# Base's logits inside the W_out products, Cm folded into the state matrices, and a new order of rows, ids and gathers

## The chip, the core and the metric

The kernel runs on one core of a Trainium2 chip. Its engines work side by side, each through its own queue of instructions in order: TensorE (PE, matmuls; PEld is its weight loads), VectorE (DVE), ScalarE (ACT), GpSimd (POOL) and SyncE (SP, which only issues DMA transfers here). The metric is the device time of one launch in microseconds.

## The reference, cut to what matters

There are 8 sequences of 512 tokens with 256 features. Each passes a modulated layer norm and a state-space block, and then a modulated layer norm and a mixture of 8 experts in which each token uses one expert.

```
mod = (silu(c) @ wmod) -> sa, ca, ga, sb, cb, gb      # per sequence; ga, gb kept away from 0
h = layernorm(x) * (1 + ca) + sa
xn = layernorm(h) * gamma + beta;  u, z = split(xn @ W_in.T)
xc = silu(causal_conv4(u) + conv_b)
state_t = state_{t-1} @ A.T + u_t @ Bm.T              # 16 states
y_t = (xc_t + state_t @ Cm) * sigmoid(z_t)
x = x + ga * (h + y @ W_out.T)
h = layernorm(x) * (1 + cb) + sb
logits = h @ wr + br;  gate = p1 / (p1 + p2);  e = argmax(logits)
x = x + gb * gate * (gelu(h @ w1[e] + b1[e]) @ w2[e] + b2[e])
```

All of it is float32. The profile shows one float32 matmul as two instructions, each with its weight load.

## The kernel before, in words

**The plan.** The kernel does not issue instructions as it builds them. A class `Plan` records each one with the tiles it reads and writes, a supposed length and a due time (`nc.due`), and `order` (L191) lays them out as a list schedule: always the instruction that could start first, the earlier due time deciding between equals. The result fixes the order of instructions on every engine's queue, SP's included. What a DMA is supposed to take after its issue stands in `order`: 3.5 us for an indirect one (a gather or scatter on GpSimd's queue), bytes over a shared wire of 300 GB/s for another, and 2.2 us of reach behind either. On the chip, semaphores make an instruction wait for its inputs, and everything behind it on the same engine waits too. Two plans follow each other, the sequences' and the experts'; all of the first is emitted ahead of the second. In the profile nearly every instruction carries the line of the recorder, L159, or L154 for further matmuls of one group.

**The first plan** makes the matrices of `states` and `vectors` and then works on sequence after sequence: `stage_norm` (both layer norms, `xnT`, the normalized rows with features on partitions), `stage_base` (`base` = x + ga h, its transpose `baseT`, W_out times ga as `wb_` with 8 further columns `wr2` that yield logits), `stage_conv`, `stage_out`, `stage_place`. The stages of neighbouring sequences overlap as the plan decides.

The states are computed in chunks of 4 tokens. `stage_conv` puts the inputs of the states into `v` [128, 128] (position in the chunk by state on partitions, chunk on columns), sums over chunks by products `pd`, turns `v` into all states `s` by four products with `lq` (`pst`) and a copy on ScalarE, and does the convolution in `sv`. `stage_out` multiplies `s` with Cm: `cmt` holds four pieces of Cm at partitions 0, 32, 64 and 96, and two products `pc` of 32 rows run side by side. VectorE adds them to `sv` and multiplies by the gate, and `po` is the product with `wb_`: 256 columns of output and 8 of logits. The part of the logits that comes from `base` is a product of its own in `stage_base`, `pl`, copied to `bl` and added to the logits `lg`.

`stage_place` writes the rows `xr` of the sequence to `xp_d` in DRAM (L933, on SP; on ScalarE's queue for the last sequence), next to modulation rows that SP has copied there. It counts each token's place in its expert's list and scatters token numbers to `ids_d` with four indirect DMAs.

**The experts** work in slots of 256 tokens (128 for some) of one expert. `name_tokens` (L1047) loads a slot's token numbers from `ids_d` to `ids` on SP; `expert_of` (L1059) loads the expert's w1, b1, b2 and w2 on SP (2.1 MB); `rows_of` gathers the rows to `xg` on GpSimd's queue; `features` normalizes and modulates them in `hg` and transposes them (`tp`) to `hT`; `layer1` gives `ph` and, through the gelu, `gl`; `layer2` gives `py` and `ot`, which is scattered to the output. The slots 0 to 2 are named after six sequences, when the lists already hold three full blocks, and slot 0's first layer belongs to the first plan. The other slots need all eight sequences: a table on VectorE ends in `ei`, which holds their experts and places. Weights of three slots are fetched ahead (four buffers). The ids of the first four late slots are loaded before the slots' loop `work` (L1313), all others in its first turn.

Of the kernel before, what the change touches and what calls it, by code (L numbers as in the profile page):

```python
# [10 lines left out]
FP = mybir.dt.float32  # L11
I32 = mybir.dt.int32
AF = mybir.ActivationFunctionType
ALU = mybir.AluOpType
# [21 lines left out]
class Plan:  # L36
# [154 lines left out]
    def order(self):  # L191
# [34 lines left out]
        while len(order) < len(ops):  # L226
# [63 lines left out]
def adaln_mamba_moe_kernel(  # L290
# [71 lines left out]

    cmt = cpool.tile([P, P], FP, name="cmt")
    nc.gpsimd.memset(cmt, 0.0)
# [69 lines left out]
    with tc.tile_pool(name="wa", bufs=1) as wa, tc.tile_pool(  # L434
# [32 lines left out]
        for j in range(KI):  # L467
            nc.sync.dma_start(out=cmt[32 * j : 32 * j + DS, :], in_=cm[:, j * P : (j + 1) * P])
# [124 lines left out]
        def states():  # L593
# [16 lines left out]

            lt = wa.tile([DS, CH, P], FP, name="lt")
# [72 lines left out]
            return lq, wb, lm, bw  # L684
# [81 lines left out]
        def stage_base(t):  # L766

            b, xt, bc, h = (t[k] for k in ("b", "xt", "bc", "h"))
            base = h
            nc.gpsimd.tensor_tensor(base, base, rows(bc[:, 2, :]), ALU.mult)  # L770
            nc.gpsimd.tensor_tensor(base, base, xt, ALU.add)
            wb_ = a2.tile([P, KI, D + E], FP, name="wb_")
            nc.gpsimd.tensor_tensor(
                wb_[:, :, 0:D], wo, bc[:, 2, :].unsqueeze(1).to_broadcast([P, KI, D]), ALU.mult
            )
            nc.gpsimd.tensor_copy(wb_[:, :, D:], wr2[:, :, b, :])
            baseT = a2.tile([P, KD, L], FP, name="baseT")
# [11 lines left out]
            t.update(base=base, wb_=wb_, bl=bl)  # L789

        def stage_conv(t):
# [4 lines left out]
            v = a2.tile([P, NC], FP, name="v")  # L796
# [52 lines left out]
            t.update(s=s, sv=sv)  # L849

        def stage_out(t):


            b, xnT, s, sv, base, wb_, bl = (
                t[k] for k in ("b", "xnT", "s", "sv", "base", "wb_", "bl")
# [3 lines left out]
            for g in range(KI // 2):  # L859
                pair = (2 * g, 2 * g + 1)  # L860
                tz, pc = {}, {}
                for j in pair:
                    tz[j] = a3.tile([P, L], FP, name=f"tz_{b}_{j}", tag="tz")
                    with nc.wanting([tz[j]]):
                        px = project(xnT, b, KI + j)
                    nc.scalar.activation(tz[j], px, AF.Tanh, scale=0.5)
                with nc.wanting(done=[sv[:, j, :] for j in pair]), nc.side_by_side():
                    for j in pair:
                        pc[j] = ps_x.tile([P, L], FP, name=f"pc_{b}_{j}", tag="px")
# [4 lines left out]
                for j in pair:  # L874
                    nc.vector.tensor_tensor(sv[:, j, :], sv[:, j, :], pc[j], ALU.add)
                    nc.vector.scalar_tensor_tensor(
                        y2[:, j, :], tz[j], 1.0, sv[:, j, :], ALU.add, ALU.mult
                    )
# [44 lines left out]
        def stage_place(t):  # L923
# [9 lines left out]
            (nc.sync if b < B - 1 else nc.scalar).dma_start(  # L933
# [125 lines left out]
        def expert_of(i, w1t, w2t, b1t, b2t):  # L1059
# [16 lines left out]
            loads(fn, [w1t, b1t, b2t, w2t], [number], 2.5)  # L1076
# [44 lines left out]
        lq, wb, lm, bw = states()  # L1121
        rw, rsum, wr2 = vectors()
        for b in range(B):
# [6 lines left out]
            if b == FEW - 1:  # L1130
# [6 lines left out]
                for i in range(2):  # L1137
# [15 lines left out]
                    epool.tile([P, D], FP, name="b2_0"),  # L1153
# [8 lines left out]
    with tc.tile_pool(name="g", bufs=2) as gp, tc.tile_pool(  # L1162
# [150 lines left out]
        def work(slots, got, begun=None):  # L1313
# [27 lines left out]
        late = slots[NEARLY:]  # L1341
        for i in late[:FIRST]:
            name_tokens(i)
# [65 lines left out]
```

## Time and profile before

| | |
|---|---|
| three runs | 624.2, 630.1, 630.36 us; median 630.1 |
| the profiled execution | 630.57 us, its span 628.8 |
| TensorE | busy 578.3 us, mean granted clock 0.941 |
| VectorE, ScalarE, GpSimd | busy 355.0, 211.5, 212.8 us |
| DMA | 96.72 MB, 154 GB/s over the span |
| setup, then sequences | up to about 62 us, then to 336; first `po` groups of the eight at 77.8, 115.6, 147.7, 183.3, 219.6, 254.1, 289.2, 329.0 us |
| experts | first layer of slot 0 at 336.6, last matmul near 615 us |

The page's first part gives each engine's busy time; the second shows the span in 40 slices, with the clock that was granted to TensorE; the groups and waits give, for an engine's idle time, the instruction or transfer that ended it. A timeline row is start, length, engine, line, operation, output and inputs, with the idle time before it in brackets. In rows of SPq an entry's length is the time that SyncE needed for the issues, not the transfer's.

### The profile page before, as it was taken

The numbers are of one execution on the slowest core, as the hardware profiler recorded it, in microseconds if no ns is written. First come the engines' busy times: TensorE is split into PE (matmuls) and PEld (weight loads), VectorE is DVE, ScalarE is ACT, GpSimd is POOL, SyncE is SP. The second block draws the span as 40 slices with busy tenths as digits, with TensorE's granted clock in tenths as the row PEclk, the third lists the DMA queues.
The fourth block names the chain that finished last, engine by engine and source line by source line (L and its number), as shares of the span: only waits on it lengthen the run. The fifth ranks groups of instructions, "written<-read, shape, count | busy, mean of one in ns | idle before, by whom it ended". The sixth has DMA issues, their size and how long they took to land. (4 is left out here: it accounts for less than half of the span.)

```text
span 628.8 us, 8434 instructions
## 1 busy us (share of the span) xinstructions
PE 578.3 (92%) x2754; PEld 422.4 (67%) x2754; DVE 355.0 (56%) x1101; ACT 211.5 (34%) x408; POOL 212.8 (34%) x335
## 2 busy tenths in 40 slices
PE   5899999999999999999699865899999999999991
PEld 2456565656475665656358755688988988988980
DVE  6869589598968678476396612353342541542210
ACT  2227244354463445351252211121322223322320
POOL 1603562735344364530322312333332233321101
PEclk9859699899989799998999996899999999999996
DMA  8268996220301001010814995999887877882000
GB/s 289 88 165 227 261 269 137 37 75 0 94 0 35 1 2 35 0 36 0 269 44 121 189 203 167 342 389 358 284 276 241 297 242 263 282 303 90 24 4 16
DMA packets 58799, 96.72 MB, mean 154 GB/s; under 512 B 9900, under 2 KB 41966, under 8 KB 58752
## 3 DMA queue, kind: packets, MB, share of 16 engines
q1 hardware_dynamic: 50288, 72.44, 39.2%
q0 software_dynamic: 7936, 23.17, 10.5%
q10 hardware_dynamic: 528, 0.53, 0.8%
q8 instruction: 23, 0.38, 0.3%
q14 instruction: 24, 0.20, 0.2%
HBM read 86.42 MB, written 22.81 MB: 174 GB/s over the span
## 5 line engine op out<-in xcount | busy, mean ns | idle before, releaser
L159 ACT ACTIVATE gl<-ph,b1t 128x256 f32<-128x256 f32 (+1 forms) x152 | 68.6, 451 | 191.9 <-PE ph L154 189.9
L154 PE MATMUL py<-w2t,gl 128*128 128x256 f32 x476 | 108.5, 380 | 0.1
L154 PEld LDWEIGHTS py<-w2t,gl 128*128 128x128 f32 x476 | 90.5, 190 | 12.6 <-issue 0.5
L159 POOL DMA_INDIRECT out<-ot,ids x36 | 38.0, 1055 | 160.2 <-DVE ot L159 151.4
L159 PE MATMUL ph<-hT,w1t 128*128 128x256 f32 (+1 forms) x304 | 85.2, 362 | 0.0
L154 PE MATMUL ph<-hT,w1t 128*128 128x256 f32 (+1 forms) x304 | 84.8, 361 | 0.0
L159 PE MATMUL px<-xnT,wi 128*128 128x512 f32 x128 | 77.4, 689 | 0.0
L159 DVE SCALAR_TENSOR_TENSOR sv<-u,pt,sv 128x512 f32<-128x512 f32 x96 | 71.5, 758 | 4.0 <-ACT sv L159 4.0
L154 PE MATMUL px<-xnT,wi 128*128 128x512 f32 x128 | 71.9, 646 | 0.0
L159 DVE TENSOR_TENSOR ot<-py,b2t 128x256 f32<-128x256 f32 x34 | 14.4, 423 | 92.6 <-PE py L154 92.6
L159 POOL DMA_INDIRECT xg<-xp_d,ids x36 | 37.1, 1031 | 70.6 <-DMA ids<-ids_d 49.5
L154 PEld LDWEIGHTS ph<-hT,w1t 128*128 128x128 f32 x304 | 56.0, 193 | 6.5
L159 PEld LDWEIGHTS ph<-hT,w1t 128*128 128x128 f32 x304 | 55.8, 195 | 5.7
L159 POOL DMA_INDIRECT ids_d<-tok,row x32 | 37.0, 1156 | 54.9 <-DVE row L159 30.6
L154 PEld LDWEIGHTS px<-xnT,wi 128*128 128x128 f32 x128 | 26.9, 210 | 35.1 <-issue 35.1
L159 DVE TENSOR_SCALAR hg<-xg 128x256 f32<-128x256 f32 x36 | 15.0, 418 | 60.0 <-DMA xg<-xp_d,ids 60.0
L159 ACT COPY u<-px 128x512 f32<-128x512 f32 x32 | 18.7, 583 | 69.1 <-PE px L154 69.1
L159 ACT ACTIVATE tz<-px 128x512 f32<-128x512 f32 x32 | 19.1, 596 | 57.8 <-PE px L154 55.1
L159 PEld LDWEIGHTS px<-xnT,wi 128*128 128x128 f32 x128 | 22.5, 205 | 23.6 <-issue 18.0
L159 POOL TENSOR_TENSOR rs<-ve,nhalf 128x4 f32<-128x4 f32 x16 | 20.0, 1250 | 43.5 <-DVE ve L159 23.9
L159 DVE TENSOR_TENSOR xr<-po,h 128x256 f32<-128x256 f32 x32 | 13.5, 423 | 31.0 <-PE po L154 28.4
L159 DVE TENSOR_TENSOR hg<-hg,xg 128x256 f32<-128x256 f32 x72 | 28.6, 421 | 0.9
(360 smaller groups left out, 955.3 us busy)
## 6 DMA issues: line engine op xcount, KB each, us to landing
w1t<-in_w SPq DMA_DIRECT2D x19, 1024.0 KB, 7.6
w2t<-in_w SPq DMA_DIRECT2D x19, 1024.0 KB, 5.9
xp_d<-modb_d SPq DMA_DIRECT2D x8, 1536.0 KB, 29.1
xt<-in_x SPq DMA_DIRECT2D x8, 512.0 KB, 6.9
xp_d<-xr SPq DMA_DIRECT2D x7, 520.0 KB, 3.5
bc<-mod_d SPq DMA_DIRECT2D x7, 384.0 KB, 5.1
b2t<-in_b SPq DMA_DIRECT2D x19, 128.0 KB, 7.3
w<-in_w SPq DMA_DIRECT2D x2, 1024.0 KB, 8.9
```

Source lines behind the costliest of these rows:

```text
L154: me["calls"].append(lambda: getattr(getattr(self.nc, name), op)(*args, **kw))
L159: calls=[lambda: getattr(getattr(self.nc, name), op)(*args, **kw)],
```

## The change

- Indirect DMAs count 9.0 us in the plan, not 3.5.
- `cs` takes the place of `lq` and `s`: the matrices of `states` are multiplied with Cm once, in the setup (four products with 512 columns, four copies on ScalarE), and `pc` is four full products of `cs` and `v` for each quarter of the channels. `cmt` is loaded once, [16, 512]. There are no pairs side by side any more; `v` has three buffers.
- `pl`, `bl` and their copy go; the products of `baseT` and `rw` are accumulated on the last 8 columns of `po`, and `lg` is a copy.
- The last sequence's `xr` is written from SP like the others.
- In the plan, slot 0's weights stand behind the early gathers.
- One late slot's ids are loaded before the loop; in each turn the next slot's ids are loaded ahead of the weights that are fetched in it.

```diff
-                    end += 3.5
+                    end += 9.0
...
-        for j in range(KI):
-            nc.sync.dma_start(out=cmt[32 * j : 32 * j + DS, :], in_=cm[:, j * P : (j + 1) * P])
+        cmt = wa.tile([DS, DI], FP, name="cmt")
+        nc.sync.dma_start(out=cmt, in_=cm)
...
-            i4 = wa.tile([DS, P], FP, name="i4")
-            nc.vector.memset(i4, 0.0)
-            for q in range(P // SP):
-                nc.vector.tensor_copy(i4[:, q * SP : q * SP + DS], i16)
-            pq = ps_s.tile([P, CH, P], FP, name="pq", tag="ps")
+            cs = wa.tile([P, CH, DI], FP, name="cs")
             for i in range(CH):
-                nc.tensor.matmul(pq[:, i], lhsT=lt[:, i, :], rhs=i4, start=True, stop=True)
-            lq = wa.tile([P, CH, P], FP, name="lq")
-            nc.vector.tensor_copy(lq, pq)
+                pq = ps_x.tile([P, DI], FP, name=f"pq_{i}", tag="px")
+                nc.tensor.matmul(pq, lhsT=lt[:, i, :], rhs=cmt, start=True, stop=True)
+                nc.scalar.copy(cs[:, i, :], pq)
...
-            pl = ps_t.tile([P, NT, E], FP, name="pl", tag="tp")
-            bl = a3.tile([P, NT, E], FP, name="bl")
-            with nc.wanting([bl]):
-                for n in range(NT):
-                    for k in range(KD):
-                        nc.tensor.matmul(
-                            pl[:, n, :], lhsT=baseT[:, k, n * P : (n + 1) * P],
-                            rhs=rw[:, k, 0, b, :], start=(k == 0), stop=(k == KD - 1),
-                        )
-            nc.vector.tensor_copy(bl, pl)
...
-            v = a2.tile([P, NC], FP, name="v")
+            v = a3.tile([P, NC], FP, name="v")
...
-            pst = ps_s.tile([P, L], FP, name=f"pst_{b}", tag="ps")
-            s = a2.tile([P, L], FP, name="s")
-            with nc.wanting([s]):
-                for i in range(CH):
-                    nc.tensor.matmul(
-                        pst.rearrange("p (c i) -> p i c", i=CH)[:, i, :], lhsT=lq[:, i, :], rhs=v,
-                        start=True, stop=True,
-                    )
-            nc.scalar.copy(s, pst)
...
-                        nc.tensor.matmul(
-                            pc[j], lhsT=cmt[j * SP : (j + 1) * SP, :],
-                            rhs=s[j * SP : (j + 1) * SP, :], start=True, stop=True,
-                        )
...
+            for j in range(KI):
+                tz = a3.tile([P, L], FP, name=f"tz_{b}_{j}", tag="tz")
+                with nc.wanting([tz]):
+                    px = project(xnT, b, KI + j)
+                nc.scalar.activation(tz, px, AF.Tanh, scale=0.5)
+
+                pc = ps_x.tile([P, L], FP, name=f"pc_{b}_{j}", tag="px")
+                with nc.wanting(done=[sv[:, j, :]]):
+                    for i in range(CH):
                         nc.tensor.matmul(
+                            pc.rearrange("p (c i) -> p i c", i=CH)[:, i, :],
+                            lhsT=cs[:, i, j * P : (j + 1) * P], rhs=v, start=True, stop=True,
                         )
+                nc.vector.tensor_tensor(sv[:, j, :], sv[:, j, :], pc, ALU.add)
...
                             po, lhsT=y2[:, j, n * P : (n + 1) * P], rhs=wb_[:, j, :],
-                            start=(j == 0), stop=(j == KI - 1),
+                            start=(j == 0), stop=False,
+                        )
+
+                    for k in range(KD):
+                        nc.tensor.matmul(
+                            po[:, D:], lhsT=baseT[:, k, n * P : (n + 1) * P],
+                            rhs=rw[:, k, 0, b, :], start=False, stop=(k == KD - 1),
                         )
...
-                nc.vector.tensor_tensor(lg[:, n, :], po[:, D:], bl[:, n, :], ALU.add)
+                nc.vector.tensor_copy(lg[:, n, :], po[:, D:])
...
-            (nc.sync if b < B - 1 else nc.scalar).dma_start(
+            nc.sync.dma_start(
                 out=xp_d[b * L : (b + 1) * L, 0:OWN].rearrange("(n p) c -> p n c", p=P), in_=xr
...
-        def expert_of(i, w1t, w2t, b1t, b2t):
+        def expert_of(i, w1t, w2t, b1t, b2t, behind=()):
...
-            loads(fn, [w1t, b1t, b2t, w2t], [number], 2.5)
+            loads(fn, [w1t, b1t, b2t, w2t], [number, *behind], 2.5)
...
-                    epool.tile([P, D], FP, name="b2_0"),
+                    epool.tile([P, D], FP, name="b2_0"), pre,
...
+                if n + ahead + 1 < len(slots):
+                    name_tokens(slots[n + ahead + 1])
                 if n + ahead < len(slots):
                     got.append(fetched(slots[n + ahead]))
...
-                    for i in late[FIRST:]:
-                        name_tokens(i)
...
-        late = slots[NEARLY:]
-        for i in late[:FIRST]:
-            name_tokens(i)
+        name_tokens(slots[NEARLY])
```

More of the change, by code (lines that the diff above doesn't have):

```diff
@@ L361, in adaln_mamba_moe_kernel @@
     at = cpool.tile([DS, STEPS, 2, DS], FP, name="at")
-    cmt = cpool.tile([P, P], FP, name="cmt")
-    nc.gpsimd.memset(cmt, 0.0)
     brt = cpool.tile([P, E], FP, name="brt")
@@ L682, in states @@
             nc.vector.tensor_copy(bw[:, :, 0:DS], pb)
-            return lq, wb, lm, bw
+            return cs, wb, lm, bw
         def stats(src, b, which, rs=None, nm=None):
@@ L778, in stage_base @@
             to_features(baseT, base, None, None, f"b{b}")
-            pl = ps_t.tile([P, NT, E], FP, name="pl", tag="tp")
-            bl = a3.tile([P, NT, E], FP, name="bl")
-            with nc.wanting([bl]):
-                for n in range(NT):
-                    for k in range(KD):
-                        nc.tensor.matmul(
-                            pl[:, n, :], lhsT=baseT[:, k, n * P : (n + 1) * P],
-                            rhs=rw[:, k, 0, b, :], start=(k == 0), stop=(k == KD - 1),
-                        )
-            nc.vector.tensor_copy(bl, pl)
-            t.update(base=base, wb_=wb_, bl=bl)
+            t.update(base=base, wb_=wb_, baseT=baseT)
         def stage_conv(t):
@@ L848, in stage_conv @@
                 nc.scalar.activation(cv, cv, AF.Silu)
-            t.update(s=s, sv=sv)
+            t.update(v=v, sv=sv)
         def stage_out(t):
-            b, xnT, s, sv, base, wb_, bl = (
-                t[k] for k in ("b", "xnT", "s", "sv", "base", "wb_", "bl")
+            b, xnT, v, sv, base, wb_, baseT = (
+                t[k] for k in ("b", "xnT", "v", "sv", "base", "wb_", "baseT")
             )
             y2 = sv
[L859 to L869, printed above, removed]
+            for j in range(KI):
[6 more added lines that the diff above has]
+                    for i in range(CH):
@@ L870, in stage_out @@
                         nc.tensor.matmul(
-                            pc[j], lhsT=cmt[j * SP : (j + 1) * SP, :],
-                            rhs=s[j * SP : (j + 1) * SP, :], start=True, stop=True,
-                        )
[L874 to L877, printed above, removed]
-                    )
+                            pc.rearrange("p (c i) -> p i c", i=CH)[:, i, :],
@@ L880, in stage_out @@
+                            lhsT=cs[:, i, j * P : (j + 1) * P], rhs=v, start=True, stop=True,
+                        )
+                nc.vector.tensor_tensor(sv[:, j, :], sv[:, j, :], pc, ALU.add)
+                nc.vector.scalar_tensor_tensor(
+                    y2[:, j, :], tz, 1.0, sv[:, j, :], ALU.add, ALU.mult
+                )
             xr = rowp.tile([P, NT, OWN], FP, name="xr")
@@ L888, in stage_out @@
                             po, lhsT=y2[:, j, n * P : (n + 1) * P], rhs=wb_[:, j, :],
-                            start=(j == 0), stop=(j == KI - 1),
+                            start=(j == 0), stop=False,
+                        )
+                    for k in range(KD):
+                        nc.tensor.matmul(
+                            po[:, D:], lhsT=baseT[:, k, n * P : (n + 1) * P],
+                            rhs=rw[:, k, 0, b, :], start=False, stop=(k == KD - 1),
                         )
                 nc.vector.tensor_tensor(x1[:, n, :], po[:, 0:D], base[:, n, :], ALU.add)
-                nc.vector.tensor_tensor(lg[:, n, :], po[:, D:], bl[:, n, :], ALU.add)
+                nc.vector.tensor_copy(lg[:, n, :], po[:, D:])
             rs, nm = stats(x1, b, 2, xr[:, :, D], xr[:, :, D + 1])
@@ L1120, in adaln_mamba_moe_kernel @@
         PERIOD = 36.0
-        lq, wb, lm, bw = states()
+        cs, wb, lm, bw = states()
         rw, rsum, wr2 = vectors()
```

## The prediction

> **What bounds the kernel now.** I read the page first, then the table of stretches, then TensorE's timeline around every stretch in which it idled or ran slowly, then those of SyncE and the DMA queues. A page line gives busy time, share and instructions; PEclk is the granted clock in tenths for 40 slices of 15.7 us.
>
> ```profile
> span 628.8 us, 8434 instructions
> ...
> PE 578.3 (92%) x2754; PEld 422.4 (67%) x2754; DVE 355.0 (56%) x1101; ACT 211.5 (34%) x408; POOL 212.8 (34%) x335
> ...
> PEclk9859699899989799998999996899999999999996
> ```
>
> TensorE is busy 92% and no other engine above 56%, so time is lost where TensorE idles or is slowed: the dips in PEclk. There are three kinds.
>
> **First**, half clock while TensorE is busy. The table of stretches, 3.41 us each (busy time of TensorE, its weight loads, VectorE, ScalarE, GpSimd; then PEclk, DMA share, GB/s):
>
> ```profile
> 144.44:147.85 3.41, 3.41 (x24) 2.71 (x23) 3.41 (x8) 0.60 (x1) 0.68 (x3) 1.00 0.01 0
> 147.85:151.26 3.41, 3.41 (x18) 2.90 (x17) 1.11 (x9) 3.37 (x7) 1.10 (x3) 1.00 0.00 0
> ...
> 175.16:178.57 3.41, 3.41 (x28) 2.56 (x24) 3.41 (x11) 1.62 (x3) 2.60 (x6) 0.99 0.01 0
> 178.57:181.98 3.41, 3.41 (x7) 1.18 (x4) 2.39 (x8) 0.00 (x0) 1.18 (x6) 0.51 0.00 0
> ```
> and TensorE's timeline in the third (start, length, operation):
> ```profile
> 174.60 0.69 PE L159 MATMUL pc<-s,cmt 32*128 32x512 f32 x1
> ...
> 175.66 0.33 PE L159 MATMUL tp_a<-ident,xn 128*128 128x128 f32 x1
> ...
> 176.15 0.29 PE L159 MATMUL pl<-rw,baseT 128*128 128x8 f32 x2
> ...
> 177.94 0.69 PE L159 MATMUL pc<-s,cmt 32*128 32x512 f32 x1
> ```
>
> The stretch ahead of the drop is busy throughout, but filled with `pl` (8 columns) and `pc` (32 rows). Drops of this part start at 65.9, 110.3, 178.6, 212.7, 250.2 and 284.4, whole multiples of 3.41 us apart, each behind `pl` next to `pc` (the first behind `pl` next to `pr`, 64 columns). From 144.44 to 147.85, `pl` has 1.7 of 3.41 us with px beside it, and no drop follows: half a stretch of thin products is borne, four fifths are not (246.8 to 250.2: 1.75 of `pl`, 1.06 of `pc`).
>
> **Second**, the logits of sequence 6, 298 to 311 us (bracket: idle before, releaser):
>
> ```profile
> 302.31 1.05 POOL L159 DMA_INDIRECT xg<-xp_d,ids  x1 [18.80 <-DMA ids<-ids_d]
> ...
> 307.31 1.05 POOL L159 TENSOR_TENSOR xr<-ve,nhalf 128x4 f32<-128x4 f32 x1
> ...
> 309.37 0.41 DVE L159 TENSOR_SCALAR hg<-xg 128x256 f32<-128x256 f32 x1 [11.05 <-DMA xg<-xp_d,ids]
> ...
> 311.27 0.39 PE L159 MATMUL pd<-v,lm 32*32 32x120 f32 x2 [4.72 <-DVE v L159]
> ```
>
> The plan counts 3.5 us for a gather; these landed after 8.0 (median). So GpSimd stands before its gathers with the pow that VectorE needs queued behind them, VectorE stands before `hg`, and TensorE idles for v.
>
> **Third**, the passage to the experts:
>
> ```profile
> 345.71 0.42 ACTq L159 DMA_DIRECT2D xp_d<-xr  x1
> ...
> 360.99 0.70 PE L159 MATMUL py<-w2t,gl 128*128 128x256 f32 x2 [2.61 <-DMA w2t<-in_w]
> ...
> 368.83 0.33 SPq L1052 DMA_DIRECT2D ids<-ids_d  x1
> ...
> 373.53 15.05 SPq L1052 DMA_DIRECT2D ids<-ids_d  x14
> ...
> 383.62 0.47 PE L159 MATMUL tp<-ident,hg 128*128 128x128 f32 x1 [11.79 <-DVE hg L159]
> ...
> 400.90 0.45 PE L159 MATMUL tp<-ident,hg 128*128 128x128 f32 x1 [3.02 <-DVE hg L159]
> ```
>
> Slot 3's ids are read only at 368.8, when the last scatters (issued to 348.9) are in, after up to 19.7 us. Then 14 id loads hold SyncE until 388.6, ahead of slot 4's weights. The last xr lands after 23.0 us from ScalarE's queue; the other seven take 3.5 from SyncE's. From 420 to 610 TensorE has no gap.
>
> **The change, part by part.** The profiled execution took 630.57 us (span 628.8 and 1.8 around it), 0.5 above the median of the runs, 630.1.
>
> *Cm folded in.* Before, per sequence: `pst`, 8 instructions from 172.68 to 173.57, 0.89, and `pc` twice 1.06 (174.60 to 175.66): 3.01. After: 16 products of two instructions, shaped like pst's, 32 x 0.111 = 3.56. So +0.55, times 8: **+4.4**, all on TensorE. ScalarE loses eight copies of 0.585 and v reaches pc without it; ScalarE is 34% busy: 0. v gets a third buffer for its longer life. The Trainium skill speaks against this step: its page TensorEngine Tiling (Array Packing), section Overview, has up to four products of at most 32 rows share the array. By that factor pc would have cost 8 x 0.43 / 4 = 0.86 and the step 8 x (3.56 - 0.89 - 0.86) = +14.5; the trace has 1.06 for two products of a pair, and decides.
>
> *Setup.* `pq` (8 instructions, 1.08 us from 55.77) becomes 8 of 512 columns at px's pitch of 0.43: 3.44, **+2.4**; 0 if it falls into a gap, +5 at the half clock of 32 to 45 us. VectorE is rid of i4 and the lq copy (0.68), ScalarE gets four copies of 0.58, four cm loads (3.07 us of SyncE) become one. None of these ends a wait there: 0.
>
> *Base's logits in po.* The 16 instructions (176.15 to 177.94) move between the po's at the same 0.11 each: 0, bounds -1 (a group start of 0.1 less per sequence) and +2 (0.06 more per output tile). VectorE's bl copy goes (8 x 0.18) and an add becomes a copy, hidden under its idle 44%. baseT now lives until po, as wb_ of two buffers does already: 0.
>
> *The clock.* `pl` is spread, 0.45 us behind each 1.77 of po (a fifth thin), and pc is dense, so no stretch of `pl` beside thin `pc` is left. Slow times: 10.4 us from 65.9, 6.9 from 212.7, 3.4 at the four others; half of each is lost: 5.2 + 3.45 + 4 x 1.7 = 15.4. I take **-13**, since `pr` stays thin in the first; bounds 0 and -15.4.
>
> *3.5 to 9.0.* A scatter, an id load and a gather follow each other, so the plan puts the id loads 5.5 us and `hg` 11 us later; hg was 11.05 late. VectorE then does v and pd first, and GpSimd can serve the pow ahead of some gathers. Gone would be 4.72 of idling and 1.7 lost to the half clock from 312. Two gathers may still stand ahead of the pow: **-5**, bounds 0 and -6.4. Slot 0's weights, now planned behind the gathers, fall behind sequence 6's xr (314.3) and land 8.9 later: 323, needed at 336.6: 0. Behind the last xr (345.7) slot 0 would start some 17 later.
>
> *The passage.* xr is emitted on SyncE ahead of slots 1 and 2, so it waits there for VectorE until 345.6, and behind it wait slot 1's weights (issued at 337.1 before), slot 2's and slot 3's ids. 0.52 + 1.05 MB at 380 GB/s (346 to 350: 379, 357) is 4.1 us, plus 1.8 (what a lone xr takes beyond its 1.4): 351.9, needed at 351.1. Wait 0.8. The other 3.15 MB are in at 360; the scatters land 9.0 to 11.8 after 348.9 (those between 165 and 250 us): 361. Only one id load then stands before weights: ids 4.5 more, gather 2.6 + 8.0, hg 1.3: 377.5. TensorE's own work (four groups of 6.95) lasts to 379.7. Slot 3 starts near 381, not 401.4: -20, of which 17.4 is idling (2.61 + 11.79 + 3.02) and the rest slow clock. This cover is 2 us thin and rests on 380 GB/s, where 350 to 368 moved 114 on average with two queues waiting; at 114 the same chain gives 402, +1. I take **-13**, two thirds of the way, bounds -20 and +27 (rival 1). Later id loads go out one slot before their gather: 4.5 + 8.0 fit into a slot of 14, three slots ahead of use: 0.
>
> Sum: 4.4 + 2.4 - 13 - 5 - 13 = -24.2; 630.6 - 24.2 = **606**.
>
> **Rivals.** (1) *Slower: the loads crawl behind xr.* If the scatters and not ScalarE's queue caused the crawl of 350 to 368, it now meets xr and all 4.2 MB of weights, where 3.4 MB were through by 350 before. Slot 3 starts at 346 + 4.72 MB/rate + 15; that outweighs the other terms (-11.2) below 91 GB/s. At 70 (352 to 356 had 66 and 31) it starts at 428, +27: 646. For it: no row shows scatters beside xr and weights in one queue. Against: scatters beside 1.5 MB copies left these 140 to 186 GB/s at 104 to 110.
> (2) *The ids bound the passage anyway*, at 114 GB/s or with landings of 16.6 to 19.7 as now: 630.6 - 11.2, **619**.
> (3) *The drops are not the thin products'.* Then the 13 stay: **619**. Against: six drops of six stand behind them. The Trainium skill, page TensorE: Matmul & The Clock Gate, section Why this matters for your kernels, warns of gaps of over 3 us without matmuls. By that alone these drops would have no cause that the change removes; the trace has TensorE busy 3.41 of 3.41 ahead of them.
> (4) *The plan changes but not the order on the chip*, since queues and semaphores decide: only clock and products count, 630.6 - 13 + 6.8 = **624**.
>
> **Chances.** Forecast 0.56 (its own range 592 to 614); (1) 0.16, of it 0.11 slower and 0.05 unchanged; (2) 0.13; (3) 0.07; (4) 0.08, half of it unchanged. A measurement of this kernel tells about 1%, 6.3 us, from no change. Faster 0.80, within it 0.09, slower 0.11. The range reaches from all gains, 630.6 + 4.4 + 1 - 15.4 - 6.4 - 20 - 2 = 592, to 630, and leaves out mostly the slower part of (1).
>
> **What would show it.** PEclk at 1.00 from 110 to 290; po groups 33 us apart (289.2 - 183.3 is 3 x 35.3 now); no wait of 11 us of VectorE for xg; the last xr landing in under 6 us; no wait of over 4 us at slot 3's tp. Drops behind stretches without thin products, or w1t of slot 1 landing 12 us after the last xr's issue, would prove me wrong.

## The result, and the profile after

| | before | changed |
|---|---|---|
| runs beside each other (four each) | 624.2 to 630.36 us, median 628.4 | 602.82 to 606.44 us, median 605.6 |
| ratio, 95% interval | | 0.962 [0.955, 0.969] |
| profiled execution, its span | 630.57, 628.8 us | 602.82, 601.0 us |

The sum of the prediction came out, 606 against 605.6, but not by its terms. The two profiled executions lie 27.8 us apart and the medians 22.8, because the one before was the slowest of its four and the changed one the fastest; what follows is read from these two, so its parts add up to 5 us more than the medians differ by. The page of the changed kernel:

```profile
span 601.0 us, 8691 instructions
...
PE 563.9 (94%) x2882; PEld 430.1 (72%) x2882; DVE 351.4 (58%) x1087; ACT 210.5 (35%) x404; POOL 209.3 (35%) x334
...
PEclk9779999999999999999999977999999999999996
```

From the fourth slice to the 23rd the clock stands at 9 (nine tenths or more); what is left of the half clock is in the setup (second and third slice) and in the 24th and 25th, the passage to the experts. The table of stretches, with the cuts at the first `po`, the last sequence's `po` and the first `py` of slot 3. Columns: length, then busy time of TensorE, its weight loads, VectorE, ScalarE, GpSimd, then PEclk, DMA share, GB/s. Before:

```profile
0.00:77.75 77.75, 66.67 (x331) 37.26 (x331) 57.57 (x191) 29.29 (x50) 27.44 (x61) 0.82 0.70 206
77.75:328.95 251.20, 243.20 (x1105) 148.37 (x1103) 187.87 (x595) 109.33 (x197) 109.24 (x202) 0.95 0.24 65
328.95:409.69 80.74, 63.33 (x288) 54.46 (x288) 33.51 (x133) 16.12 (x35) 21.26 (x21) 0.92 0.80 204
```

After:

```profile
0.00:71.98 71.98, 63.33 (x335) 35.67 (x335) 56.35 (x184) 31.98 (x55) 25.65 (x60) 0.91 0.71 200
71.98:304.57 232.59, 229.91 (x1215) 156.36 (x1211) 183.74 (x585) 105.09 (x189) 107.17 (x195) 1.00 0.29 78
304.57:381.44 76.87, 65.35 (x304) 55.62 (x303) 38.47 (x145) 16.28 (x34) 23.61 (x29) 0.91 0.76 213
```

The front (the first two rows) is 24.4 us shorter, the passage 3.9, and the steady slots behind it as long as before (219.1 and 219.6). Time lost to the clock is length times one less PEclk, added up over stretches of a quarter of a microsecond, since the column above is rounded: in the front 13.65 + 11.95 before and 6.8 after, so -18.8. Idle time is length less busy time: 11.1 + 8.0 before, 8.65 + 2.7 after, so -7.7. The rest, work, is +2.1.

Not all of the front is firm. Six of the experiments below (e5, e6, e9, e10, e12 and e13) change nothing in the order of the first plan, and their first `po` begins anywhere from 69.98 to 75.84 us, while from there to the last sequence's `po` they all take 232.2 to 232.7. So the 18.6 us between the first and the last `po` (251.2 before, 232.6 after) stand, and the 5.8 us ahead of the first `po` can't be told from the spread of single executions.

The wait in sequence 6 is gone. GpSimd's rows there:

```profile
285.41 1.00 POOL L159 DMA_INDIRECT xg<-xp_d,ids  x1 [0.31 <-issue]
286.44 1.06 POOL L159 TENSOR_TENSOR xr<-ve,nhalf 128x4 f32<-128x4 f32 x1
287.69 1.06 POOL L159 DMA_INDIRECT xg<-xp_d,ids  x1 [0.19 <-issue]
```

The pow (the row with `nhalf`) now stands behind two of the four gathers, and VectorE's `hg` behind the work on v. TensorE waits there under 1 us.

The passage, rows of SyncE's queue, GpSimd, VectorE and TensorE from one timeline (the length of an SPq row is the time of its issues):

```profile
318.68 0.38 SPq L1041 DMA_DIRECT2D w1t<-in_w  x1
...
323.01 0.38 SPq L159 DMA_DIRECT2D xp_d<-xr  x1
...
341.93 1.43 SPq L1028 DMA_DIRECT2D ids<-ids_d  x2
...
352.62 22.88 SPq L1028 DMA_DIRECT2D ids<-ids_d  x13
```

```profile
326.25 0.98 POOL L159 DMA_INDIRECT ids_d<-tok,row  x1 [0.30 <-issue]
...
346.60 1.05 POOL L159 DMA_INDIRECT xg<-xp_d,ids  x1 [11.78 <-DMA ids<-ids_d]
...
357.32 0.41 DVE L159 TENSOR_SCALAR hg<-xg 128x256 f32<-128x256 f32 x1 [13.05 <-DMA xg<-xp_d,ids]
```

```profile
348.54 0.59 PE L154 MATMUL ph<-hT,w1t 128*128 128x256 f32 x2
358.71 0.48 PE L159 MATMUL tp<-ident,hg 128*128 128x128 f32 x1 [9.57 <-DVE hg L159]
...
364.16 1.06 PE L159 MATMUL py<-w2t,gl 128*128 128x256 f32 x2
```

Slot 1's weights go out ahead of xr, not behind it. Slot 3's ids are read at 341.9, 15.7 us after the last scatter's issue (326.25). Its gathers are issued from 346.6 and land 10.7 us later, while the weights of slots 3 and 4 move, at 400 GB/s from 352 on. TensorE stands 9.57 us before slot 3's `tp`, and half clock follows to 368. Slot 2's second layer (`py`, 364.16) stands behind these transposes in TensorE's queue, so it can't fill the wait.

### The profile page after: what moved, and what is told of

Read it like the earlier page. It is cut to its first block, busy times and chain, and to the rows that moved or that the text cites. A ratio compares the mean times of both kernels' runs of the same rounds, so it can differ in the third digit from the quotient of the medians.

```text
span 601.0 us, 8691 instructions
## 1 busy us (share of the span) xinstructions
PE 563.9 (94%) x2882; PEld 430.1 (72%) x2882; DVE 351.4 (58%) x1087; ACT 210.5 (35%) x404; POOL 209.3 (35%) x334
## 5 line engine op out<-in xcount | busy, mean ns | idle before, releaser
L154 PE MATMUL py<-w2t,gl 128*128 128x256 f32 x476 | 109.8, 383 | 0.0
L154 PEld LDWEIGHTS py<-w2t,gl 128*128 128x128 f32 x476 | 91.7, 193 | 12.9
L159 DVE SCALAR_TENSOR_TENSOR sv<-u,pt,sv 128x512 f32<-128x512 f32 x96 | 77.2, 809 | 12.7 <-ACT sv L159 12.4
L154 PE MATMUL ph<-hT,w1t 128*128 128x256 f32 (+1 forms) x304 | 84.2, 359 | 0.0
L159 PE MATMUL px<-xnT,wi 128*128 128x512 f32 x128 | 69.6, 626 | 0.0
L154 PE MATMUL px<-xnT,wi 128*128 128x512 f32 x128 | 65.9, 597 | 0.0
L154 PEld LDWEIGHTS ph<-hT,w1t 128*128 128x128 f32 x304 | 55.6, 191 | 6.3
L159 POOL DMA_INDIRECT xg<-xp_d,ids x36 | 37.8, 1051 | 60.9 <-DMA ids<-ids_d 40.5
L159 POOL DMA_INDIRECT ids_d<-tok,row x32 | 34.8, 1087 | 36.1 <-DVE row L159 13.7
L154 PEld LDWEIGHTS px<-xnT,wi 128*128 128x128 f32 x128 | 24.6, 192 | 31.2 <-issue 31.2
L159 DVE COPY hT<-tp 128x512 f32<-128x512 f32 (+1 forms) x20 | 12.7, 634 | 36.3 <-PE tp L154 28.1
L159 PEld LDWEIGHTS px<-xnT,wi 128*128 128x128 f32 x128 | 21.3, 192 | 16.4 <-issue 14.8
```

Of the source, the lines that this page charges most:

```text
L154: me["calls"].append(lambda: getattr(getattr(self.nc, name), op)(*args, **kw))
L159: calls=[lambda: getattr(getattr(self.nc, name), op)(*args, **kw)],
```

## The experiments

A kernel that moves instructions is ordered anew by the plan, and the order around the passage falls differently each time. So each run is read in two parts: where the last sequence's `po` begins, and how long the span goes on from there.

| kernel | median us | ratio to before, 95% | last po begins | from there |
|---|---|---|---|---|
| before | | | 329.5 | 299.3 |
| changed | 605.6 | 0.962 [0.955, 0.969] | 305.0 | 296.0 |
| e1 logits apart | 651.8 | 1.039 [1.033, 1.045] | 359.2 | 290.9 |
| e2 Cm in pairs | 606.1 | 0.967 [0.961, 0.972] | 310.5 | 293.5 |
| e3 3.5 us | 615.5 | 0.981 [0.975, 0.987] | 315.3 | 297.5 |
| e4 last xr on ScalarE | 600.6 | 0.958 [0.951, 0.965] | 304.9 | 295.0 |
| e5 no last xr write | 599.4 | 0.957 [0.952, 0.961] | 305.1 | 289.7 |
| e6 no last scatters | 593.4 | 0.947 [0.942, 0.951] | 308.8 | 285.3 |
| e7 orders only | 616.9 | 0.985 [0.981, 0.990] | 324.8 | 289.7 |
| e8 products only | 605.1 | 0.966 [0.963, 0.968] | 307.0 | 297.3 |
| e9 slot 2 behind scatters | 603.4 | 0.962 [0.957, 0.968] | 308.8 | 298.5 |
| e10 also slot 4 held | 604.3 | 0.959 [0.952, 0.967] | 307.5 | 296.4 |
| e12 most weights held | 595.2 | 0.950 [0.944, 0.957] | 304.6 | 289.3 |
| e13 slot 3 behind its gather | 606.3 | 0.970 [0.962, 0.979] | 303.0 | 298.4 |

The last two columns, in us, are of the profiled execution and count from the further matmuls of `po` (L154), half a microsecond behind the cut above; by what is said above of the setup, a few us between two rows of the fourth column mean nothing. The kernel before was run again beside each group of experiments, with medians from 625.2 to 628.4.

### Which product ends the half clock: e1, e2, e7, e8

e1, the logits apart again:

```diff
+            pl = ps_t.tile([P, NT, E], FP, name="pl", tag="tp")
... (16 products, the copy to bl, and the add to lg, as before)
-                        nc.tensor.matmul(
-                            po[:, D:], lhsT=baseT[:, k, n * P : (n + 1) * P],
...
```

> The changed kernel with base's logits again as a group of their own (pl, copied to bl, added to lg). Theory A (the half clock comes from thin products following one another: pl beside the pairs of pc in 32 rows, so either of the two folds is enough to end it): pl now stands next to pc products of 128 rows, the clock stays full from 41 to 354 us, the time is within 2 us of the changed kernel (604 to 608 us, ratio 0.96). Rival B (the logits' products alone bring it): six or so drops come back in the front, 2 us each, 615 to 619 us.

e2, `lq`, `s` and the pairs of 32 rows again, the logits still in `po`:

```diff
-                for i in range(CH): nc.tensor.matmul(pc..., lhsT=cs[:, i, j * P : (j + 1) * P], rhs=v, ...)
+                nc.tensor.matmul(pc[j], lhsT=cmt[j * SP : (j + 1) * SP, :], rhs=s[j * SP : (j + 1) * SP, :], ...)
```

> The changed kernel with s = lq v and the pairs of pc in 32 rows again, the logits still in po. Theory A (both kinds of thin product must lie side by side): no drop from 41 to 354 us, and since s and the pairs took less time than sixteen products with cs, about 4 us less than the changed kernel: 600 to 603 us. Rival C (the pairs of pc alone bring the half clock): drops come back in the front, 2 us each, 608 to 615 us. Rival B (the logits alone do it) expects what A does here.

e7, the kernel before with the orders alone, and e8, the changed kernel with the orders of before; in e8:

```diff
-                    end += 9.0
+                    end += 3.5
...
-            nc.sync.dma_start(
+            (nc.sync if b < B - 1 else nc.scalar).dma_start(
...
-                    epool.tile([P, D], FP, name="b2_0"), pre,
+                    epool.tile([P, D], FP, name="b2_0"),
...
-                    name_tokens(slots[n + ahead + 1])
... (ids as before; e7 is the reverse of all this in the kernel before)
```

> The kernel before with the orders alone: 9.0 us planned for an indirect transfer, xr always on SP, slot 0's weights behind its gathers, ids one slot ahead; the logits and the product with Cm as before. My theory: the wait for xg in sequence 6 goes (about 6 us), but the half-clock stretches of the front stay, each behind pl beside pc in 32 rows: five or more from 110 to 290 us, and the passage gains 0 to 4 us: 616 to 623 us. Rival (the clock in the front follows the orders, not the products): no half clock from 110 to 290 us, 604 to 610 us.

> The changed kernel with the orders of before: the logits in po and cs v for the product with Cm, but 3.5 us planned for an indirect transfer, the last xr on ScalarE, slot 0's weights not held, ids as before. My theory: no half clock from 110 to 280 us, the stall in sequence 6 is there (10 us, as with 3.5 in the changed kernel), the passage about as before: 613 to 620 us. Rival (the orders did the whole gain): 624 to 632 us.

The four combinations of the two products, read where TensorE doesn't idle:

- neither fold (e7): half clock from 177.5, 211.5, 245.5, 279.5 and 320.5 us, each behind `pl` beside `pc` in 32 rows, TensorE busy or nearly so ahead of it;
- logits in `po`, thin pairs (e2): from 110 to 320 none;
- logits apart, dense `pc` (e1): from 160 to 380 one, at 243, behind 1.93 and 0.22 us of idling around two small products;
- both (changed, e8): none from the setup up to the passage, in e8 up to 343.

Two stretches of 3.41 us in e7, the one that holds `pl` and both pairs of `pc` and the one that follows:

```profile
207.73:211.14 3.41, 3.41 (x23) 2.46 (x24) 2.19 (x7) 1.63 (x3) 2.80 (x7) 1.00 0.02 1
211.50:214.91 3.41, 3.41 (x6) 1.41 (x5) 2.56 (x5) 0.00 (x0) 0.38 (x6) 0.51 0.00 0
```

and two in e1, the first with the same `pl`, beside `px`:

```profile
215.35:218.76 3.41, 3.41 (x24) 2.75 (x23) 3.38 (x7) 0.60 (x1) 1.82 (x2) 1.00 0.15 28
218.76:222.17 3.41, 3.41 (x17) 2.90 (x16) 0.79 (x5) 1.80 (x4) 1.16 (x4) 1.00 0.89 44
```

TensorE is busy 3.41 of 3.41 us in all four; what differs is how much of the first is thin. The drops of a run begin whole multiples of 3.41 us apart. Counted from the timelines on that grid (thin: `pl`, `pc` in 32 rows, and the small products of the counts and of `pd`), thin products fill 2.6 to 3.4 us of the stretch ahead of each of these five drops of e7. Where TensorE idles for less than 0.3 us and no drop follows, they fill at most 2.4 us of a stretch in e2 (only `pc`), 1.9 in e1 (nearly only `pl`), and 1.2 in the changed kernel and e8. So in this kernel neither kind alone fills enough of a stretch; the drops come where both stand side by side, and either fold alone ends them. Whether the two kinds weigh the same, no run shows. The prediction named the neighbourhood but had both folds share the credit. e1 missed its range of 604 to 608, but its time is no price of the logits: its plan put the seven modulation copies of the setup at 80.9 us instead of 41.8, and TensorE idles 35 us from 79 to 152. e2 came out above its 600 to 603, with waits of its own.

e8 has the whole gain by itself: 605.1. The orders alone give 9.8 us (e7, 626.8 beside it), and on top of the products nothing that can be told. I had expected 613 to 620 for e8, since I thought that the 3.5 us would bring back the wait in sequence 6; e7 came out in its range of 616 to 623.

### The plan's time for a gather: e3

```diff
-                    end += 9.0
+                    end += 3.5
```

> The changed kernel with 3.5 us instead of 9.0 planned for an indirect transfer. My theory: the pow of sequence 6 stands behind all four gathers of slots 0 and 1 on GpSimd again, VectorE waits some 10 us for xg in sequence 6, TensorE idles 4 to 5 us there: 609 to 611 us. Rival: the 9.0 does nothing for the front and its loss goes elsewhere (the gathers are waited for at the end of the front instead): 604 to 607 us.

615.5, 9.9 us above the changed kernel, twice what I had taken. All of it lies ahead of the last `po` (315.3 against 305.0): four gathers, then the pow, VectorE before `hg` (5.24 and 3.40 us), TensorE idle 8.8 us in all between the `po` of sequence 6 and the last (0.7 in the changed kernel), and half clock from 296 to 303.5, which costs its work some 2 us more. Two rows of e3 and two of e8, which has 3.5 us too:

```profile
289.19 1.21 POOL L159 TENSOR_TENSOR xr<-ve,nhalf 128x4 f32<-128x4 f32 x1
...
298.36 0.60 PE L159 MATMUL pd<-v,lm 32*32 32x120 f32 x2 [6.52 <-DVE v L159]
```

```profile
284.58 1.05 POOL L159 TENSOR_TENSOR xr<-ve,nhalf 128x4 f32<-128x4 f32 x1 [15.04 <-DVE ve L159]
291.39 1.11 POOL L159 DMA_INDIRECT xg<-xp_d,ids  x1 [5.77 <-DMA ids<-ids_d]
```

In e8 the pow comes first, since the gathers are planned later there, behind slot 0's weights; TensorE waits 1.4 us. I read from this that with the new products 3.5 us hurts where the weights are put behind the gathers, as the change does, and that the 9.0 mostly repairs what another of its orders would bring. It is not shown: e8 differs from e3 in the last xr and the later ids too, and the kernel before had the wait without that order.

### What makes the loads crawl: e4, e5, e6

e4:

```diff
-            nc.sync.dma_start(
+            (nc.sync if b < B - 1 else nc.scalar).dma_start(
```

> The changed kernel with the write of the last sequence's xr from ScalarE's queue, as before. My prediction's step (the crawl of the loads in the passage is tied to that queue): the loads crawl worse and the first gathers of the whole run come later, 613 to 620 us. Rival, which the changed kernel's trace speaks for (106 to 120 GB/s from 330 to 336 us with no load on ScalarE's queue): the queue of this write costs nothing, 604 to 607 us, and the loads crawl as they do now.

600.6: below both of the expected ranges, not slower, and its interval overlaps that of the changed kernel. The loads crawl as they did (54 to 124 GB/s from 330 to 336 us), whichever queue writes xr, so ScalarE's queue was not the cause. The wait falls elsewhere here: 7.79 us for slot 1's `w2t` at 343 and 1.30 at slot 3's `tp`.

e5 and e6 keep the order of all other instructions and leave out one transfer each; in e5 the write of the last sequence's rows (and sequence 6's are written to that place too), in e6 the last four scatters:

```diff
+            if b == B - 1:
+                plan.ops[-1]["calls"].clear()
```

> The changed kernel, all instructions in the same order, without the transfer of the last sequence's rows (xr) to xp_d; instead the rows of sequence 6 are also written to that place one sequence earlier, so the last sequence's tokens get the values of the one before. Theory X (the loads crawl from 328 to 340 us because the rows of xr are being written): no crawl, the weights of slots 1 and 2 land at 300 GB/s or more by 333 us and the scatters of the last ids land by 331, slot 3's gather starts some 8 us earlier, 590 to 597 us. Rival S (the crawl is the four scatters of ids): the crawl stays, since the scatters do, 602 to 606 us.

> The changed kernel, all other instructions in the same order, without the four scatters of the last sequence's ids (its tokens are missing in the lists). Theory S (the crawl is the scatters, and slot 3 waits for their landing): the loads run at 300 GB/s or more until the weights of slots 1 and 2 are there, the id load of slot 3 no longer waits until 342 us but follows the table at 332, its gather comes 8 us earlier and TensorE doesn't stop at tp of slot 3: 585 to 592 us. Rival X (the crawl is the write of xr): the rate from 328 to 336 stays near 110 GB/s, the id load of slot 3 still goes out at 332 since it waits for nothing else, and the time is 590 to 600 us. The rate in 328 to 336 tells them apart, not the time.

The stretch from 332 to 336 us in the changed kernel, e5 and e6, last column GB/s:

```profile
332.00:336.00 4.00, 4.00 (x22) 3.48 (x21) 3.40 (x13) 2.37 (x5) 2.05 (x2) 1.00 1.15 119
```

```profile
332.00:336.00 4.00, 4.00 (x21) 3.51 (x20) 3.51 (x13) 2.27 (x5) 2.05 (x2) 1.00 0.73 69
```

```profile
332.00:336.00 4.00, 4.00 (x20) 3.54 (x19) 3.63 (x13) 1.60 (x4) 0.00 (x0) 1.00 1.07 319
```

Without xr the loads crawl, without the scatters they don't. (The front of e6 ran 3.8 us later; four microseconds on, from 336 to 340, it still moves 336 GB/s.) Four scatters of 128 numbers of 4 bytes hold up the loads. The loads hold up the scatters as well: in the quiet front the packets of four scatters issued from 197.4 to 203.1 us are all gone by 204, in the passage those of the last four (issued from 322.3 to 326.25) run on until 338, and the id load behind them goes out at 341.9. The longest wait at slot 3's `tp` falls in e6 from 9.57 to 1.43 us, and the part behind the last `po` by 10.7; its time, 593.4, is just above the 585 to 592 expected.

The write of xr is not free all the same. e5's time, 599.4, fits neither of its ranges (590 to 597, 602 to 606), and the part behind the last `po` is 6.3 us shorter in its profiled execution than in the changed kernel's: slot 3's ids are read at 339.4, 13.1 us after the last scatter's issue instead of 15.7, and the wait at `tp` is 5.63 us instead of 9.57. So xr is among the transfers that hold up the scatters, though the crawl of the loads is not its doing.

### Moving loads and scatters apart: e9, e10, e12, e13

e9, a read of one id holds slot 2's weights on SP until the scatters have landed:

```diff
-        got = [slot0, fetched(1, pre[1])] + [fetched(i) for i in range(2, NEARLY)]
+        got = [slot0, fetched(1, pre[1]), fetched(2, None, (landed, ids_d[0:1, :]), id_views[-NT:])]
...  (in expert_of, ahead of w1t)
+                hold and chip.sync.dma_start(out=hold[0], in_=hold[1])
```

> The changed kernel, order kept, but SP reads one id back from ids_d (4 bytes) ahead of slot 2's weights, so that their loads start when the last scatters have landed. Theory S (4-byte scatters and loads hold each other up; alone the scatters land within a few us of their issue, as in the quiet stretches from 197 to 205 us): the read comes back by 332 us, w1t and w2t of slot 2 land by 339 at 350 GB/s or more, ahead of their use at 343; the id load of slot 3 goes out with its table at 337 instead of 342; the wait at slot 3's tp falls from 9.6 us to under 5: 593 to 599 us. Rival (the scatters take their 12 to 15 us whatever runs beside them): the read comes back at 338 to 342 us, slot 2's weights are late, TensorE waits for them some 5 us, and the time is 605 to 612 us.

The rival, in the mechanism: the read goes out at 344.2, 14.2 us after the last scatter's issue (330.0; the whole front runs 4 us later here). The median, 603.4, is a little under the rival's 605 to 612; the profiled execution, 609.2, was the slowest of the five. Slot 1's weights and xr, 2.7 MB, still ran beside the scatters, at 35 to 91 GB/s from 334 to 340. TensorE waits 1.8 and 1.1 us for weights and 9.8 at slot 3's `tp`.

e10, besides:

```diff
+            loads(fn, [ids[:, i, 0:jb]], [at_, *id_views[: FEW * NT], *behind], 0.8)
...
+                    name_tokens(slots[n + ahead + 1], [got[-1][1]])
...  (slot 4's weights behind a read of slot 3's xg)
```

> As e9, and SP also waits for slot 3's gathered rows before it issues slot 4's weights, with the id loads no longer in one burst but each behind the weights of the slot before. If the gather of slot 3 is late because two slots' weights take the DMA engines at 400 GB/s beside it (10 us from issue to landing), it now lands within 5 us, the wait at slot 3's tp goes, and the time is 3 to 6 us below e9: 588 to 595 us. Rival (holding slot 4's weights only moves the wait to slot 4's ph): within 2 us of e9, or above it.

604.3, within 2 us of e9, as the rival has it, and not the 588 to 595 that I expected. Slot 3's weights alone, issued at 346 and 348, keep the DMA engines at 351 to 379 GB/s from 350 to 360; the gather, issued at 352.7, is waited for 7.8 us in that time.

e12, slot 1's loads in two parts, so that only the end of `w1t` and xr run beside the scatters:

```diff
+            if part:
+                expert_of(i, w1t, None, b1t, b2t)
+                expert_of(i, None, w2t, None, None, id_views[-NT:], (landed, ids_d[0:1, :]))
```

> The changed kernel with slot 1's loads in two parts: w1t and the biases as now, at 319 us, then xr, then the read of one id from ids_d that waits for the last scatters, and only then slot 1's w2t and all of slot 2's weights. Beside the scatters run only the end of w1t and xr (0.5 MB), a fifth of what ran there in e9. Theory S (scatters are slow because loads run beside them, and the loads because of the scatters): the read is back by 332 us, slot 1's w2t lands by 336, about when its py wants it, slot 2's weights by 341, slot 3's ids are read at 337: 592 to 600 us. Rival (the last four scatters need 12 us or more whatever the loads do): the read is back at 338 us or later, TensorE waits 4 us or more for w2t of slot 1 and again for slot 2, 606 to 614 us.

595.2, in the range expected and the fastest of the kernels that leave nothing out: its four runs, 593.67 to 595.6, lie below all four of the changed kernel. The DMA engines in e12, and the one wait that is left:

```profile
328.00:332.00 4.00, 4.00 (x20) 3.54 (x19) 4.00 (x14) 1.80 (x4) 0.00 (x0) 1.00 0.07 7
```

```profile
340.48 1.19 PE L159 MATMUL py<-w2t,gl 128*128 128x256 f32 x2 [5.45 <-DMA w2t<-in_w]
```

Only the end of xr crawls (61 GB/s from 326 to 327): from 328 to 332 the mean share of the DMA engines is under a tenth, and by 330 the packets of the scatters are through. The read of the id goes out at 333.8 all the same, 8 us after the last issue (325.8), later than the 332 that I gave; from 330 to 333 the DMA engines do nothing. So slot 1's `w2t` comes 5.45 us late, and half clock follows from 337 to 344.5. At slot 3's `tp` nothing is waited for any more. The stall has moved and shrunk: idle time in the passage is 6.7 us (76.90 from 304.10 to 381.00, busy 70.21) where the changed kernel had 11.5.

e13, slot 3's weights behind its gathered rows (a read of two numbers of `xg`), ids one at a time:

```diff
+            if wait:
+                held = tab.tile([1, JB], FP, name="held")
+                t = expert_of(t[0], t[1], t[2], t[3], t[4], [xg], (held, xg[0:1, :, 0]))
```

> The changed kernel with slot 3's weights behind slot 3's gathered rows on SP (a read of two of its numbers waits for them), and the id loads no longer in one burst. If the gather of slot 3 takes 10 us from issue to landing because the weights of slots 3 and 4 run beside it at 400 GB/s, it lands within 5 us here, the transposes of slot 3 come at 350 us instead of 358.7, w1t is there at 353, TensorE idles 4 us less and the half clock behind the idle time is shorter: 595 to 601 us. Rival (the gather takes its 8 to 10 us alone too): slot 3's weights come only at 360 us, TensorE waits for w1t instead of tp, 606 to 612 us.

Both were half right. The gather, issued at 346.5, lets slot 3's `tp` begin at 352.2 after 1.18 us of waiting: 5.7 us, where the changed kernel had 12.1 beside two slots' weights, so it does land faster without them. But the plan put the ids of slot 5 behind three more slots' weights, and the wait came back there:

```profile
396.29 0.45 PE L159 MATMUL tp<-ident,hg 128*128 128x128 f32 x1 [5.78 <-DVE hg L159]
```

The time, 606.3, is no better than the changed kernel's; it falls into the rival's range, but not for the rival's reason. e12 with e13's hold was not tried, nor a hold that ends when the scatters' packets do.

## Why the prediction was right, and where it was wrong

*Cm folded in.* The term holds: `pc` took 3.66 us a sequence, from 196.10 to 199.76, against 3.56 in the sum, so +5.2 instead of +4.4. The rule of the page TensorEngine Tiling (Array Packing), section Overview, in the Trainium skill would have put it at +14.5 by its factor of four; this kernel ran two products side by side, not four. The trace doesn't bear that price out: in e2, which packs again, a pair still takes 1.06 us, as before. The time of e2, 606.1, can't tell more, since its front has other waits: 245.7 us from the first `po` to the last against 232.6, with a stall of 2.4 us at 98.5 and 3.4 lost to the clock behind it.

*Setup.* +2.4 for `pq` can't be checked. The eight products took 0.69 us each (median), two of them at half clock, and the first `po` comes 5.8 us earlier all the same, with 6.8 us less lost to the clock there. Of these, 5.1 are the first drop of the prediction's list, at 65.9, which is gone; the other 1.7 come from the setup's older slow stretches (18 to 21.5 and 31.5 to 45.5 before, 20 to 27 and 33.5 to 40.5 after), whose cost varies with no change of the order: 6.8 us in the changed kernel, 5.1 in e13, 12.0 in e6 and e9. This is the spread of the first `po` named above, and why it varies, no run shows. The first drop's 5.1 is not in that spread: none of these kernels has one there.

*Base's logits in po.* Right: 0.45 us behind each tile, nothing else found. What it does beyond that is to break up the thin stretch, and e1 shows the same with `pl` left in one piece and `pc` dense.

*The clock.* The mechanism is right and the term a little small: all six drops of the list are gone, 15.4 us, the bound of the term and not its -13, since the first went too, which I had half kept for `pr`. With 1.7 behind the wait in sequence 6, which the next term has, and the 1.7 of the setup that no term has, this is the -18.8. Rival 3 falls: e7 against e1, e2 and the changed kernel differ in the products alone as to this. The Trainium skill's page TensorE: Matmul & The Clock Gate warns of gaps of over some 3 us without matmuls (section Why this matters for your kernels). The traces agree as to long gaps (9.57 us at slot 3's `tp`). They also show half clock behind a gap of 1.93 us with small products after it (e1), shorter than the page's, and, as in the stretches of e7 above, behind thin products in a row without any gap.

*3.5 to 9.0.* The wait is gone, and the half clock behind it. Taking the 9.0 away again costs twice the -5 (e3: 9.9). The likely reason, argued above and not shown, is that the order of slot 0's weights, costed at 0, makes the 9.0 necessary.

*The passage.* Here the prediction failed: -13 against -3.9. The step that cost most is the cover, "TensorE's own work (four groups of 6.95) lasts to 379.7". Slot 2's second layer, the fourth group, stands behind slot 3's transposes in TensorE's queue: `ph` ends at 349.1, `tp` is next at 358.71, and `py` comes at 364.16. Slot 1's two groups and most of slot 2's first layer are all the cover there is, some 6 us less than forecast. (The row at 383.62 in the prediction's own lines are these transposes; the 401.4 that it takes for slot 3's start is behind the next slot's, at 400.90.) The second step is the landing of the scatters, put at 12.1 us after the last issue (348.9 to 361): slot 3's ids were read 15.7 us after it, with the loads beside the scatters (8 us after it where most loads are held, e12). The last scatters were also issued 1.8 us later after the last sequence's first `po` (21.7 us, 19.9 before). The rest of that chain was sized right: from the read of the ids to `tp` it took 16.8 us against 16.4, the gather among it 10.7 against 2.6 + 8.0. The 2.2 us of slack that the prediction had, less these 6, 3.6, 1.8 and 0.4, give the wait of 9.57 within 0.1.

Two more steps were wrong and cost nothing here. "Xr is emitted on SyncE ahead of slots 1 and 2" was read from the source; on the chip slot 1's weights went out at 318.7 and xr at 323.0. "At 380 GB/s" tied the crawl to ScalarE's queue, and it is the scatters' (e4, e5, e6). But TensorE waited for no weights in this passage. Rival 2, that the ids bound the passage anyway, is what happened in this part. Rival 1 had the cause of the crawl right, and its rate (106 to 187 GB/s from 328 to 338) stayed above the 91 where it decides.

*Signs.* Three of the five came: PEclk 1.00 from 110 to 290, `po` groups 33.2 us apart, no long wait of VectorE for xg in sequence 6. The wait at slot 3's `tp`, under 4 us in the prediction, was 9.57. The landing of the last xr is not in the page of the changed kernel. So the total is right by compensation, which is luck: in the profiled pair the front gave 13 us more than its terms, of which up to 5.8 can be the spread of the setup, and the passage 9 us less.

*Not additive.* Products -21.6 (e8), orders -9.8 (e7), both -22.8 by the medians beside them. From the first `po` to the last the orders gain 1.5 us with the old products (251.2 before, 249.7 in e7) and 1.4 with the new (234.0 in e8, 232.6 in the changed kernel), so there they do add. Behind the last `po` they gain 9.6 us with the old products (299.3 to 289.7) and 1.3 with the new (297.3 to 296.0). SyncE's loads fall otherwise around the scatters with each change of the plan, and why e7's fall so well was not tried by a run.

## What to carry to other kernels

Read an order on the chip from the issue rows of the queue, not from the source, where a plan deals instructions out; a predicted total can be right while the step that it rests on is not. Where work is to cover a wait, check that it stands ahead of the waiting instruction in the engine's queue. Where TensorE drops to half clock without idling, look for thin products that follow each other and put dense ones between them; here one of two folds was enough. Keep small scatters that something waits for away from bulk loads: a read that holds the loads back for some us took 7 us off this kernel by the ratios to the kernel before, and 10 by the medians (e12).

## What the runs showed that I had not expected

- Scatters of 4-byte numbers and 1 MB loads slow each other: the packets of 512 numbers are through within 1 us of their last issue in the quiet front, and some 12 us after it beside loads, whose rate falls from 319 to 119 GB/s (e6 and the changed kernel, 332 to 336 us). By which resource, no run shows; the DMA engines' share stays near 1 while little moves. The Trainium skill, page DMA: Bandwidth & Descriptors, section Specifications, has transfers of under 512 B done as read-modify-write; whether that is what the loads meet is open.
- A wait for scattered ids ended 8 us after the last issue although the packets were gone after 4 (e12).
- An indirect gather of two times 128 rows is used by TensorE within 6 us of its first issue when no weights run beside it (5.7, e13), and after 12 when they do (12.1, the changed kernel).
